# The query projection of a perceiver block as seven block products, with its block sums on VectorE

## The chip, the cores and the metric

The kernel runs on one core of one Trainium2 chip. The metric is the device time of one execution in microseconds (us), and lower is better. Before the change the median of three runs is 1107.33 us (1107.03 to 1108.09). The engines are called as in the profile: PE is TensorE (matmuls, with PEld for its weight loads), DVE is VectorE, ACT is ScalarE, POOL is GpSimd, and SP issues most transfers.

## The reference, cut to what matters

A block of 512 tokens, 512 wide, attends to a context of 8192 rows with 16 heads of 32; then a linear attention and a quantized feed-forward network follow. Everything is float32. The change touches only the queries of the first attention:

```python
x = x + xattn(layernorm(x), ctx_1024, ctx_1024, Wq, bq, Wk, bk, Wv, bv, Wo, bo)
# in it, with E = 512:
q = split_heads(query @ Wq + bq)      # 512 x 512 by 512 x 512
k = split_heads(key @ Wk + bk)        # 8192 x 512 by 512 x 512
v = split_heads(value @ Wv + bv)
weights = softmax(einsum('bhqd,bhkd->bhqk', q, k) / sqrt(32))
z = einsum('bhqk,bhkd->bhqd', weights, v)
```

## The kernel before, in words

The function `network` is built twice. The first copy (`exact` false) is the one that runs; the second (`exact` true) stands behind a test of a flag and is only run if the softmax's denominators fall out of their bounds. All that follows is the first copy.

The context is worked through in 16 blocks of 512 rows. Keys and values of a block are each a 512 x 512 x 512 product, made in `blockwise` (L441) as seven products of 256 x 256 x 256 blocks instead of eight (a Strassen scheme with 15 sums). `product` (L463) issues one of them in four steps, each with four matmuls of 32 output columns (`by_columns`, L385; two instructions per matmul in the profile, so 32 per product). `evict` (L487) adds a finished product into the result: on ACT for product 1 (L492), else on DVE with a plain addition (L479) or a pair of additions with the bias (L482). The products run in the order 1, 2, 6, 7, 5, 4, 3 (L527). Each takes a PSUM buffer from the pool `ps_m`, tag "pt", which has two, so a product needs the buffer of the second product before it to be evicted.

The sums that the scheme needs are made on POOL: four of a weight (`sums_of_weights`, L360, additions at L365) and four of a context block (`sums_of_ctx`, L373, additions at L383). Each is a 128x512 addition of tensors in SBUF.

The stretch around the change is straight-line code. In order: POOL gets the sums of Wk and of block 0 (L545, L546). PE makes ten matmuls of the identity, key product 1 of block 0 (L562), the transposes of the normed tokens `xn` into PSUM (L565), from where DVE and ACT copy them to `xnT` (L570, L572), and key product 2 (L573). Then come the queries (L574 to L579): for each of four groups of 128 columns `project` (L131) issues four full 128x128 matmuls of 512 columns (L136; 32 instructions in all) into a "pt" buffer, and ACT adds the bias into `qT` (L577). After that POOL gets the sums of Wv (L581), for which `place_w` takes the buffer of Wq, and the addition of `bo` to the residual (L583). The other five key products of block 0 follow on PE (L734), then `common_maxima` (L628), which reads `qT` for the first scores (L643) while the values of block 0 are made.

The helper `in_order` keeps the instructions of an engine in the order in which the code issues them. So what stands earlier in the code on DVE holds up what stands later on DVE, even where that is ready. Wq comes in one transfer of 1024 KB on SP's queue (L130), behind the halves of Wk and of context block 0.

Of the kernel before, what the change touches and what calls it, by code (L numbers as in the profile page):

```python
# [8 lines left out]
F32 = mybir.dt.float32  # L9
BF16 = mybir.dt.bfloat16  # L10
AF = mybir.ActivationFunctionType
ALU = mybir.AluOpType
# [4 lines left out]
P = 128  # L17
# [9 lines left out]
def network(  # L27
# [24 lines left out]
    nc = tc.nc  # L52
    S, E = x.shape
# [4 lines left out]
    NE = E // P  # L58
    NF = FF // P
    HG = P // D  # L60
    KB = 512
# [15 lines left out]
    def in_order(i):  # L77

        return tc.keep_in_program_order(i)
# [6 lines left out]
    for i in range(7):  # L86
        n = 1 << i
# [45 lines left out]
    def project(ps, lhsT, rhs):  # L133

        for c in range(NE):
            nc.tensor.matmul(  # L136
                ps, lhsT=lhsT(c), rhs=rhs(c), start=(c == 0), stop=(c == NE - 1)
            )
# [138 lines left out]
    ap2 = ctx.enter_context(tc.tile_pool(name="ap2", bufs=2))  # L277
    ap4 = ctx.enter_context(tc.tile_pool(name="ap4", bufs=4))
    ps_m = ctx.enter_context(tc.tile_pool(name="ps_m", bufs=2, space=PSUM))

    with ExitStack() as actx:
        aw = actx.enter_context(tc.tile_pool(name="aw", bufs=1))

        qT = aw.tile([P, NE, S], F32, name="qT")
# [11 lines left out]
        bias = aw.tile([P, NE], F32, name="bias")  # L296
# [4 lines left out]
        ct, kT, vt, tt = {}, {}, {}, {}  # L301
# [18 lines left out]
        wq_sb, wv_sb, wk_sb = place_w(), place_w(), place_w()  # L320
# [8 lines left out]
        bk_sb = load_cols(bk, NE, "bk_sb")  # L329
        load_w(Wq, wq_sb)  # L330
        bq_sb = load_cols(bq, NE, "bq_sb")
# [12 lines left out]
        xnT = ap4.tile([P, NE, S], F32, name="xnT", tag="ex")  # L344
# [11 lines left out]
        def block_of(w, i, j):  # L356

            return w[:, ts(j, NE // 2), ts(i, E // 2)]
# [79 lines left out]
                for k in range(NC) for c in range(NE)  # L438
            ]

        def blockwise(b, keys, parted=False):  # L441

            st = {"ps": {}}
            half = KB // 2

            def begin():
                if keys:
                    kT[b] = ap2.tile([P, NE, KB], F32, name="kT")  # L450
                    dst = kT[b]
                    st["C"] = {
                        (i, j): dst[:, ts(i, 2), ts(j, half)]
                        for i in range(2) for j in range(2)
                    }
                else:
                    vt[b] = ap2.tile([P, NC, E], F32, name="vt")
                    dst = vt[b]
                    st["C"] = {
                        (i, j): dst[:, ts(j, 2), ts(i, half)]  # L460
                        for i in range(2) for j in range(2)
                    }
            def product(n, m, k):  # L463
                w = (of_keys if keys else of_values)[n - 1]
                b11, _, b21, b22 = [
                    block_of(ct[b], kk, j) for j in range(2) for kk in range(2)
                ]
                t = tt[b]
                x = [b11, b21, b22, t[:, 3], t[:, 0], t[:, 1], t[:, 2]][n - 1]
                lhsT, rhs = (w, x) if keys else (x, w)  # L470
                by_columns(
                    st["ps"][n][:, m, :], lhsT[:, k, ts(m, P)], rhs[:, k, :],
                    k == 0, k == 1,
                )

            def add(dst, src, ps, i=None):

                if not keys or i is None:
                    in_order(nc.vector.tensor_tensor(dst, src, ps, ALU.add))  # L479
                    return  # L480
                for m in range(2):
                    in_order(nc.vector.scalar_tensor_tensor(  # L482
                        dst[:, m, :], ps[:, m, :], bk_sb[:, 2 * i + m : 2 * i + m + 1],
                        src[:, m, :], ALU.add, ALU.add,
                    ))

            def evict(n):  # L487
                C, ps = st["C"], st["ps"][n]

                C11, C12, C21, C22 = C[0, 0], C[0, 1], C[1, 0], C[1, 1]  # L490
                if n == 1:
                    in_order(nc.scalar.copy(C12, ps))  # L492
                elif n == 6:
                    add(C12, C12, ps)
                    if parted:
                        in_order(nc.scalar.copy(C21, C12))
                elif n == 7 and parted:
                    add(C22, C22, ps, 1)
                    add(C21, C21, ps, 1)
                elif n == 7:  # L500
                    add(C21, C12, ps, 1)
                elif n == 5 and parted:
                    add(C22, C12, ps)
                    add(C12, C12, ps, 0)
                elif n == 5:
                    add(C22, C21, ps)
                    add(C12, C12, ps, 0)
                elif n == 4:
                    add(C21, C21, ps)

                    if not keys:
                        sums_of_ctx(b + 1)
                elif n == 2:
                    add(C11, C12, ps, 0)
                elif n == 3:
                    add(C12, C12, ps)
                for i, j in {(7 if parted else 5): [(1, 1)], 4: [(1, 0)], 2: [(0, 0)], 3: [(0, 1)]}.get(n, []):
                    for m in range(2):
                        if keys:
                            made.add(("k", b, 2 * i + m, j))  # L520
                        else:
                            made.add(("v", b, 2 * j + m, i))
                if not keys and n == 3:
                    load_ctx(b + 2)

            steps = []
            for n in (1, 2, 6, 5, 3, 7, 4) if parted else (1, 2, 6, 7, 5, 4, 3):  # L527
                for m in range(2):
                    for k in range(2):
                        def step(n=n, m=m, k=k):  # L530
                            if (n, m, k) == (1, 0, 0):
                                begin()
                            if (m, k) == (0, 0):
                                ps = ps_m.tile([P, KB], F32, name="pm", tag="pt")
                                st["ps"][n] = ps.rearrange("p (a n) -> p a n", a=2)
                            product(n, m, k)
                            if (m, k) == (1, 1):
                                evict(n)
                        steps.append(step)
            return steps  # L540
# [3 lines left out]
        if not exact:  # L544
            of_keys = sums_of_weights(wk_sb)  # L545
# [3 lines left out]
        def first_keys(n):  # L549

            for step in key_steps[: 4 * n]:
                step()
            del key_steps[: 4 * n]

        with tc.tile_pool(name="ps_q", bufs=NE, space=PSUM) as ps_q:
# [12 lines left out]
            for c in range(NE):  # L568
                if c % 2 == 0:
                    in_order(nc.vector.tensor_copy(xnT[:, c, :], pts[c]))  # L570
                else:
                    in_order(nc.scalar.copy(xnT[:, c, :], pts[c]))  # L572
        first_keys(1)  # L573
        for g in range(NE):  # L574
            pq = ps_m.tile([P, S], F32, name="pq", tag="pt")
            project(pq, lambda c: wq_sb[:, c, ts(g, P)], lambda c: xnT[:, c, :])
            in_order(nc.scalar.activation(  # L577
                qT[:, g, :], pq, AF.Identity, bias=bq_sb[:, g : g + 1]
            ))  # L579
        if not exact:  # L580
            of_values = sums_of_weights(wv_sb)  # L581
        for t in range(NT):
# [8 lines left out]
        for b in range(first + 1, total):  # L591
# [5 lines left out]
            elif b < total - 1:  # L597

                steps = blockwise(b, True, True)
# [173 lines left out]
        def sums(dn, ex, start, stop):  # L773
            for j in range(HG):
                in_order(nc.tensor.matmul(
                    dn[ts(j, D), :], lhsT=ones_f, rhs=ex[:, j, :],
                    start=start, stop=stop,
                ))
# [90 lines left out]
        for i, u in enumerate(units):  # L869
            ex = weights(*u)  # L870
            if i >= last_block:
                b, g, k = u
# [25 lines left out]
            else:  # L898
# [3 lines left out]
                add = [weighted_sums(*late.pop(0)) for _ in range(len(late))]  # L902
# [116 lines left out]
    with ExitStack() as lctx:  # L1019
# [91 lines left out]
        def products(g):  # L1111


            ps = ps_m.tile([P, 2, F], F32, name="kv", tag="pt")
            for t in range(NT):
                for j in range(HG):
                    in_order(nc.tensor.matmul(
                        ps[ts(j, D), 0, :], lhsT=va[:, t, ds(g * P + j * D, D)],
                        rhs=kf[g][:, j, ts(t, F)],
                        start=(t == 0), stop=(t == NT - 1),  # L1120
                    ))
            for j in range(HG):
                in_order(nc.tensor.matmul(
                    ps[ts(j, D), 1, :], lhsT=ones_c, rhs=kf_sum[g][:, j, :],
                    start=True, stop=True,
                ))
            kvT[g] = lp.tile([P, 2, F], F32, name="kvT")
            in_order(nc.scalar.copy(kvT[g], ps))
# [215 lines left out]
    for q in range(NF // 4):  # L1344
# [14 lines left out]
        for i in range(4):  # L1359
            f = 4 * q + i  # L1360
# [7 lines left out]
            if f < 2 or i % 2 == 1:  # L1368
                k = f if f < 2 else f // 2 + 1
# [33 lines left out]
    for i in range(len(chunks) + 1):  # L1403
        if i < len(chunks):
            f, n = chunks[i]
# [4 lines left out]
        f, n = chunks[i - 1]  # L1410
# [77 lines left out]
```

## Time and profile before

| | us |
|---|---|
| median of three runs | 1107.33 |
| the profiled execution | 1107.43 |
| its span in the trace | 1105.6 |
| PE busy in the span | 1084.2 |
| DVE busy | 935.0 |
| ACT busy | 642.2 |
| POOL busy | 179.3 |
| queries on PE (L136), in the chain | 13.93, from 14.69 to 28.62 |
| the five key products after them | 8.94, from 28.62 |
| all before the chain reaches PE (start and first loads) | 9.00 |

The span is the time from the first to the last recorded instruction; the execution's own time is 1.8 us longer. "Busy" is the union of an engine's instruction times. The chain of work that ended last goes back from the last instruction to whatever released it, step by step. In rows of instructions, the duration of a single one can be longer than the distance to the next, since neighbours on an engine overlap a little.

### The profile page before, as it was taken

The page shows a single profiled execution, that of the slowest core. Times are in us where ns is not written, and L with a number is a line of the kernel's source. Part 1 is how long each engine was busy: PE and PEld are TensorE (multiplying, and loading weights), DVE is VectorE, ACT ScalarE, POOL GpSimd, SP SyncE. Part 2 cuts the span into 40 slices and gives each one's busy share as a digit, 9 for nine tenths or more (in the row PEclk, how much of TensorE's full clock was granted, in tenths as well). Part 3 has the DMA queues.
Part 4 walks back from the last instruction along what each step waited for, and adds up shares of the span by engine and source line. Part 5 has one row for each costly group of instructions (what it writes and reads, how often), then busy time and mean ns, then how long its engine had stood idle before and what let it go on. Part 6 is the DMA issues. An engine that isn't in the chain of part 4 may idle for free.

```text
span 1105.6 us, 30940 instructions
## 1 busy us (share of the span) xinstructions
PE 1084.2 (98%) x14272; PEld 409.9 (37%) x14272; DVE 935.0 (85%) x869; ACT 642.2 (58%) x434; POOL 179.3 (16%) x90
## 2 busy tenths in 40 slices
PE   8999999999999999999999999999999998999996
PEld 5443333333333333333333333333333322344342
DVE  3699999998988888888888888888889789666896
ACT  2465555566666766667665555555565666346353
POOL 3520303011403030303030302021120000013000
PEclk9999999999999999999999999999999999999998
DMA  7031212110302121212010101010101021040001
GB/s 267 14 104 41 96 56 81 59 59 31 97 31 69 52 75 31 68 59 68 30 59 2 41 2 40 2 40 2 40 2 40 2 77 39 1 190 2 1 1 42
DMA packets 24778, 55.56 MB, mean 50 GB/s; under 512 B 1984, under 2 KB 2496, under 8 KB 24384
## 3 DMA queue, kind: packets, MB, share of 16 engines
q1 hardware_dynamic: 24352, 52.97, 14.4%
q8 instruction: 114, 1.87, 0.7%
q10 hardware_dynamic: 288, 0.52, 0.1%
q14 instruction: 24, 0.20, 0.1%
HBM read 48.25 MB, written 5.24 MB: 48 GB/s over the span
## 4 chain that ended last, share of the span: by engine, by line
PE 91%; DVE 3%; ACT 3%; issue 1%; DMA 1%; SPq 0%; ACTq 0%; DVEq 0%
PE pm L388 37%; PE sc L818 24%; PE av L757 19%; ACT ex L827 3%; PE pq L1039 3%; PE po L930 1%; PE pq L136 1%; DVE unchanged L143 1%; PE pv L968 1%; PE pys L1389 1%; DMA ct<-in_ctxT 1%; DVE de L1155 1%; PE att L1144 1%; PE scm L643 0%; PE pk L388 0%
## 5 line engine op out<-in xcount | busy, mean ns | idle before, releaser
L827 ACT ACTIVATE ex<-sc,bias 128x2048 f32<-128x2048 f32 x252 | 496.3, 1970 | 339.9 <-PE sc L818 339.9
L836 DVE TENSOR_TENSOR acc<-acc,ex 128x2048 f32<-128x2048 f32 x248 | 585.0, 2359 | 67.3 <-ACT ex L827 66.7
L818 PE MATMUL sc<-qT,kT 32*64 32x512 f32 x4032 | 280.7, 613 | 4.8 <-ACT ex L827 4.8
L757 PE MATMUL av<-ex,vt 128*32 128x512 f32 x2048 | 266.9, 593 | 0.0
L383 POOL TENSOR_TENSOR tt<-ct 128x512 f32<-128x512 f32 x32 | 61.8, 1931 | 570.0 <-DMA ct<-in_ctxT 469.1
L818 PEld LDWEIGHTS sc<-qT,kT 32*64 32x64 f32 x4032 | 58.7, 129 | 217.0 <-ACT ex L827 194.4
L388 PE MATMUL pm<-w,tt 128*32 128x256 f32 x2048 | 126.8, 382 | 0.0
L388 PE MATMUL pm<-tt,w 128*32 128x256 f32 x1920 | 118.4, 382 | 0.0
L388 PE MATMUL pm<-w,ct 128*32 128x256 f32 x1536 | 96.6, 383 | 0.0
L479 DVE TENSOR_TENSOR vt<-vt,pm 128x512 f32<-128x512 f32 x112 | 75.4, 685 | 21.6 <-PE pm L388 20.6
L388 PE MATMUL pm<-ct,w 128*32 128x256 f32 x1440 | 90.3, 383 | 1.5 <-DMA ct<-in_ctxT 1.5
L388 PEld LDWEIGHTS pm<-w,tt 128*32 128x32 f32 x2048 | 59.7, 109 | 85.2 <-issue 51.8
L383 POOL TENSOR_TENSOR tt<-ct,tt 128x512 f32<-128x512 f32 x32 | 87.4, 2731 | 1.3
L757 PEld LDWEIGHTS av<-ex,vt 128*32 128x32 f32 x2048 | 65.3, 110 | 55.5 <-issue 14.0
L388 PEld LDWEIGHTS pm<-tt,w 128*32 128x32 f32 x1920 | 56.3, 109 | 78.9 <-issue 47.8
L388 PEld LDWEIGHTS pm<-w,ct 128*32 128x32 f32 x1536 | 43.6, 109 | 72.4 <-issue 47.0
L388 PEld LDWEIGHTS pm<-ct,w 128*32 128x32 f32 x1440 | 41.3, 109 | 67.3 <-issue 45.0
L479 DVE TENSOR_TENSOR kT<-kT,pm 128x512 f32<-128x512 f32 x60 | 40.9, 681 | 26.9 <-PE pm L388 26.1
L769 DVE TENSOR_TENSOR Z<-Z,av 128x512 f32<-128x512 f32 x64 | 43.4, 679 | 0.4 <-PE av L757 0.4
L482 DVE SCALAR_TENSOR_TENSOR kT<-pm,bk_sb,kT 128x256 f32<-128x256 f32 x92 | 39.9, 475 | 3.0 <-PE pm L388 1.0
L1061 ACT ACTIVATE er<-feat 128x1024 f32<-128x1024 f32 x32 | 30.2, 1029 | 11.3 <-PE feat L1083 6.4
L1067 DVE SCALAR_TENSOR_TENSOR f<-er 128x1024 f32<-128x1024 f32 x16 | 19.6, 1240 | 12.2 <-ACT er L1061 12.2
(184 smaller groups left out, 603.4 us busy)
## 6 DMA issues: line engine op xcount, KB each, us to landing
ct<-in_ctxT SPq DMA_DIRECT2D x15, 1024.0 KB, 5.3
wraw<-in_W1T SPq DMA_DIRECT2D x16, 512.0 KB, 3.8
wraw<-in_W2T SPq DMA_DIRECT2D x16, 512.0 KB, 3.8
wd<-wquant SPq DMA_DIRECT2D x16, 256.0 KB, 2.4
w_q<-wd SPq DMA_DIRECT2D x2, 2048.0 KB, 9.9
w<-in_w_qkv SPq DMA_DIRECT2D x3, 1024.0 KB, 5.0
w<-in_Wk SPq DMA_DIRECT2D x2, 512.0 KB, 6.6
ct<-in_ctxT SPq DMA_DIRECT2D x2, 512.0 KB, 7.6
```

The source lines that it names most:

```text
L383: in_order(nc.gpsimd.tensor_tensor(tt[b][:, i], x, y, ALU.subtract))
L388: in_order(nc.tensor.matmul(ps[ts(j, D)], lhsT=lhsT[:, ts(j, D)], rhs=rhs, start=start, stop=stop))
L479: in_order(nc.vector.tensor_tensor(dst, src, ps, ALU.add))
L482: in_order(nc.vector.scalar_tensor_tensor(dst[:, m, :], ps[:, m, :], bk_sb[:, 2 * i + m : 2 * i + m + 1], src[:, m, :], ALU.add, ALU.add,))
L757: in_order(nc.tensor.matmul(av[g][ts(j, D), :], lhsT=vt[b][:, k, ds(g * P + j * D, D)], rhs=ex[:, j, :], start=start, stop=stop,))
L769: in_order(nc.vector.tensor_tensor(Z[:, g, :], Z[:, g, :], ps, ALU.add))
L818: in_order(nc.tensor.matmul(sc[ts(h, P // 2), j, :], lhsT=kT[b][rows, g, ds(k * P + h * P // 2, P // 2)], rhs=qT[rows, g, :], start=not ex ...
L827: in_order(nc.scalar.activation(ex, sc, AF.Exp, bias=bias[:, g : g + 1], scale=SCALE))
L836: in_order(nc.vector.tensor_tensor(acc[:, g], acc[:, g], ex, ALU.add))
L1039: in_order(nc.tensor.matmul(ps, lhsT=wt[:, c, ts(g, P)], rhs=ynT[:, c, :], start=(c == 0), stop=(c == NE - 1),))
L1061: in_order(nc.scalar.activation(er[-1][:, d].rearrange("p a n -> p (a n)"), ps[h], function))
L1067: in_order(nc.vector.scalar_tensor_tensor(f[h], er[i][:, 0].rearrange("p a n -> p (a n)"), 1.0, er[i][:, 1].rearrange("p a n -> p (a n)"), ...
```

## The change

The queries are made by `blockwise` too, with a new flag `queries`: products of blocks of Wq with blocks of `xnT`, evicted into `qT` with the bias `bq`. The weights' sums `dw` and the tokens' sums `dx` (two tiles of the pool `ap4`, tag "ex") are eight additions of 128x512, issued on DVE between the other steps: two of the weights before key product 2, then two of the tokens, then one of each, then query products 1 and 2, then one of each again, then the other five products. The exact copy keeps the old form.

```diff
-        def blockwise(b, keys, parted=False):
+        def blockwise(b, keys, parted=False, queries=False):
...
                 if keys:
-                    kT[b] = ap2.tile([P, NE, KB], F32, name="kT")
-                    dst = kT[b]
+                    if not queries:
+                        kT[b] = ap2.tile([P, NE, KB], F32, name="kT")
+                    dst = qT if queries else kT[b]
...
             def product(n, m, k):
-                w = (of_keys if keys else of_values)[n - 1]
+                if queries:
+                    w, moving, t = of_queries[n - 1], xnT, of_tokens
+                else:
+                    w = (of_keys if keys else of_values)[n - 1]
+                    moving, t = ct[b], tt[b]
                 b11, _, b21, b22 = [
-                    block_of(ct[b], kk, j) for j in range(2) for kk in range(2)
+                    block_of(moving, kk, j) for j in range(2) for kk in range(2)
                 ]
-                t = tt[b]
...
                     in_order(nc.vector.scalar_tensor_tensor(
-                        dst[:, m, :], ps[:, m, :], bk_sb[:, 2 * i + m : 2 * i + m + 1],
+                        dst[:, m, :], ps[:, m, :],
+                        (bq_sb if queries else bk_sb)[:, 2 * i + m : 2 * i + m + 1],
                         src[:, m, :], ALU.add, ALU.add,
                     ))
...
-        first_keys(1)
-        for g in range(NE):
-            pq = ps_m.tile([P, S], F32, name="pq", tag="pt")
-            project(pq, lambda c: wq_sb[:, c, ts(g, P)], lambda c: xnT[:, c, :])
-            in_order(nc.scalar.activation(
-                qT[:, g, :], pq, AF.Identity, bias=bq_sb[:, g : g + 1]
-            ))
+        if exact:
...
+        else:
+            a11, a12, a21, a22 = [
+                block_of(wq_sb, i, j) for i in range(2) for j in range(2)
+            ]
+            b11, b12, b21, b22 = [block_of(xnT, k, j) for j in range(2) for k in range(2)]
+            of_weights, of_tokens = [
+                ap4.tile([P, 4, 2, E // 2], F32, name=f"of_{n}", tag="ex") for n in "wx"
+            ]
+            dw, dx = of_weights, of_tokens
+            of_queries = [a11, a12, dw[:, 3], a22, dw[:, 0], dw[:, 1], dw[:, 2]]
+
+            def sums(*ops):
+                for dst, x, y, how in ops:
+                    in_order(nc.vector.tensor_tensor(dst, x, y, how))
...
+            steps = blockwise(None, True, queries=True)
+
+            def products(n):
+                for _ in range(4 * n):
+                    steps.pop(0)()
+
+            add, sub = ALU.add, ALU.subtract
+            sums((dw[:, 0], a21, a22, add), (dw[:, 1], dw[:, 0], a11, sub))
+            first_keys(1)
+            sums((dx[:, 0], b12, b11, sub), (dx[:, 1], b22, dx[:, 0], sub))
+            sums((dw[:, 2], a11, a21, sub), (dx[:, 2], b22, b12, sub))
+            products(2)
+            sums((dw[:, 3], a12, dw[:, 1], sub), (dx[:, 3], b21, dx[:, 1], sub))
+            products(5)
```

Product n multiplies entry n of `of_queries` with entry n of the list in `product`: b11, b21, b22, t3, t0, t1, t2, where t is `of_tokens`. So products 1 and 2 need no sum, product 6 needs dw1 and dx1, product 7 dw2 and dx2, product 5 dw0 and dx0, product 4 dx3, and product 3 dw3.

More of the change, by code (lines that the diff above doesn't have):

```diff
@@ L518, in evict @@
                     for m in range(2):
-                        if keys:
+                        if queries:
+                            pass
+                        elif keys:
                             made.add(("k", b, 2 * i + m, j))
@@ L572, in network @@
                     in_order(nc.scalar.copy(xnT[:, c, :], pts[c]))
-        first_keys(1)
-        for g in range(NE):
-            pq = ps_m.tile([P, S], F32, name="pq", tag="pt")
-            project(pq, lambda c: wq_sb[:, c, ts(g, P)], lambda c: xnT[:, c, :])
-            in_order(nc.scalar.activation(
-                qT[:, g, :], pq, AF.Identity, bias=bq_sb[:, g : g + 1]
-            ))
+        if exact:
+            for g in range(NE):
+                pq = ps_m.tile([P, S], F32, name="pq", tag="pt")
+                project(pq, lambda c: wq_sb[:, c, ts(g, P)], lambda c: xnT[:, c, :])
+                in_order(nc.scalar.activation(
+                    qT[:, g, :], pq, AF.Identity, bias=bq_sb[:, g : g + 1]
+                ))
+        else:
[23 more added lines that the diff above has]
+            products(5)
         if not exact:
```

## The prediction

> **What bounds the kernel now.** I read the page first: busy time by engine, then the chain of work that ended last. Lines 1 and 2 show TensorE (PE) busy for 98% of the span and carrying 91% of the chain.
>
> ```profile
> PE 1084.2 (98%) x14272; PEld 409.9 (37%) x14272; DVE 935.0 (85%) x869; ACT 642.2 (58%) x434; POOL 179.3 (16%) x90
> ...
> PE 91%; DVE 3%; ACT 3%; issue 1%; DMA 1%; SPq 0%; ACTq 0%; DVEq 0%
> ```
>
> So a microsecond that PE gains or loses early is carried to the end, unless something else is late there. The change lies in the first 40 us, so next I read the chain in order of time there (start, length, what):
>
> ```profile
> 12.83 1.86 PE pm L388 x32
> 14.69 13.93 PE pq L136 x32
> 28.62 8.94 PE pm L388 x160
> ```
>
> The queries are the 13.93 us between key product 2 and the other five key products. Five products of 32 instructions take 8.94 us, 1.79 each. PE has no gap here. The table of stretches (PE, PEld, DVE, ACT, POOL busy, clock, DMA share, GB/s) says what else goes on:
>
> ```profile
> 14.60:28.60 14.00, 14.00 (x40) 6.05 (x40) 0.88 (x2) 2.06 (x3) 5.81 (x5) 1.00 0.57 199
> ```
>
> VectorE (DVE) is nearly idle, 0.88 of 14 us; GpSimd (POOL) works 5.81, and the timeline says when (start, length, engine, line):
>
> ```profile
> 10.37 5.10 POOL L365 TENSOR_TENSOR w<-w 128x512 f32<-128x512 f32 x4 [9.94 <-DMA w<-in_Wk]
> ...
> 12.54 1.29 DVE L570 COPY xnT<-pxt 128x512 f32<-128x512 f32 x2 [2.30 <-PE pxt L565]
> ...
> 14.84 0.88 DVE L482 SCALAR_TENSOR_TENSOR kT<-pm,bk_sb,kT 128x256 f32<-128x256 f32 x2 [1.02 <-issue]
> ...
> 15.41 1.27 POOL L383 TENSOR_TENSOR tt<-ct 128x512 f32<-128x512 f32 x1
> ...
> 16.77 1.27 POOL L383 TENSOR_TENSOR tt<-ct,tt 128x512 f32<-128x512 f32 x1
> ```
>
> POOL makes the key weights' sums (four) and block 0's sums (four, to 20.49) exactly where DVE is to make eight more. What that costs the trace shows later, where both engines add tensors that lie in SBUF:
>
> ```profile
> 119.96 1.28 POOL L383 TENSOR_TENSOR tt<-ct,tt 128x512 f32<-128x512 f32 x1
> 121.19 3.33 POOL L383 TENSOR_TENSOR tt<-ct 128x512 f32<-128x512 f32 x1
> 124.50 3.33 POOL L383 TENSOR_TENSOR tt<-ct,tt 128x512 f32<-128x512 f32 x1
> ```
> ```profile
> 120.56 2.83 DVE L836 TENSOR_TENSOR acc<-acc,ex 128x2048 f32<-128x2048 f32 x1
> 123.31 0.68 DVE L479 TENSOR_TENSOR kT<-kT,pm 128x512 f32<-128x512 f32 x1
> 123.91 2.78 DVE L836 TENSOR_TENSOR acc<-acc,ex 128x2048 f32<-128x2048 f32 x1
> ```
>
> Follow the ends: POOL 121.24, DVE 123.39, POOL 124.52, DVE 126.69, POOL 127.83. The steps are 2.15, 1.13, 2.17, 1.14: each ends one clean duration after the other's end. They do not run side by side; they take turns, and POOL's 3.33 is 2.2 of waiting and 1.13 of work. An instruction with a PSUM source takes no part: the key evictions at 30.55 to 33.2 keep their 0.69 and 0.88 beside POOL's L365 (28.70, four in 5.13, against 5.10 alone).
>
> **The change, step by step.** *Removed:* 32 query matmuls, 13.93 us of PE, and four ScalarE evictions of 0.69, which were beside PE. *Added on PE:* seven products at 1.79, 12.52 us. Alone that is 1.41 us gained. *Added on DVE:* eight sums of 128x512, and the evictions of six products (0.69 for an addition, 0.88 for a biased pair; pitch 0.60 and 0.86, since neighbours overlap). ScalarE evicts product 1.
>
> A sum alone costs 0.69 by the nearest row (two SBUF inputs, 128x512), 0.60 as pitch:
>
> ```profile
> L784 DVE TENSOR_TENSOR Z<-Z,acc 128x512 f32<-128x512 f32 x4 | 2.8, 692 | 0.1
> ```
>
> Taking turns, its own part is 2.17 - (2.28 - 0.69) = 0.58, scaled from the 128x2048 row (2.28 alone), and a POOL sum that goes before it costs 1.13.
>
> Three rules of the code turn DVE's time into PE waits. DVE keeps program order. The two "pt" PSUM buffers alternate, so a product waits for the eviction of the second one before it. And the sums are written ahead of evictions: dw0, dw1 (on the whole Wq) ahead of key product 2's, dx0, dx1, dw2, dx2 ahead of query product 2's, dw3, dx3 ahead of product 6's. Wq's row decides the start:
>
> ```profile
> w<-in_Wq SPq DMA_DIRECT2D x1, 1024.0 KB, 9.4
> ```
>
> Issued at 4.88, it lands at 14.28, after the xnT copies (13.83).
>
> DVE and POOL, by turns (ends in us): POOL's fourth L365 15.47; dw0 16.05; tt0 17.18; dw1 17.76; key eviction 18.6, with tt1 beside it to 18.89; dx0 19.47; tt2 20.60; dx1 21.18; tt3 22.31; dw2 22.89; dx2 23.5 (POOL is out of work); eviction of query product 2, 24.35; dw3 24.95; dx3 25.55; eviction of product 6, 26.15.
>
> PE (starts, products in the order 1, 2, 6, 7, 5, 4, 3): product 1 at 14.65; product 2 at 18.65, waiting for key product 2's buffer (2.2 idle); product 6 at 21.2, for dx1 (0.8 idle); product 7 at 24.4, for product 2's buffer (1.4 idle); product 5 at 26.2; 4 at 28.0; 3 at 29.8, its buffer free at 29.65. The rest of the keys starts at 31.6 where it started at 28.6: **+3.0 us**. The check: 1.41 gained, 4.4 of idle added.
>
> *What is moved and costs nothing.* POOL's sums of Wv wait for Wq's buffer; product 4 is its last reader, so they start at 29.8 instead of 28.70 and end at 34.9, beside five key products; values product 6 reads them first (45.05 before, 48 then). POOL's xs additions and block 1's sums follow some 1 us later, DVE then reading only PSUM. Without that cover block 1's sums would cost 1.13 a turn. The tt sums end at 22.3 instead of 20.5, needed at 31.6. Queries are read first some 8 us after the last eviction. No DMA issue is moved but behind PE.
>
> *Unknown prices.* (a) Eight sums of this shape beside POOL have no row: from 0.60 each (no turns) to 1.71 each (a turn every time); I take the turns counted above, five waits, since the L836 rows are the nearest. (b) Who goes next when both wait: if DVE kept its place for the independent pair dw2, dx2, tt3 would come behind them and in the gap of an eviction: product 7 at 23.25, end 30.7, +2.2. With hand-overs of 0.1 each, +3.8.
>
> The Trainium skill, SBUF — State Buffer, section "Who interferes with whom", says that a DVE instruction with two SBUF inputs contends with a GpSimd instruction that reads SBUF, and that the loser blocks for the whole instruction. The 2.15/1.13 steps agree; it speaks against these sums on DVE here, and against reading the overlap as half speed each, which would give +0.9. [...]
>
> (c) PE's clock is 1.00 in all stretches read, also in 5 to 9 us, where PE sat idle for 1.47. A gap of 2.2 us is not in these; I take no loss, and at worst the three gaps cost one product more, 1.8.
>
> TensorE: Matmul & The Clock Gate, Part 1, halves the clock after an idle window of about 3.4 us; by it no gap of mine would do that. If one did, an estimate from that page is 3.4 us at half speed, 1.7 us more. No row here shows it.
>
> **The rivals.**
>
> *The sums hide* (not slower). If they cost 0.60 each beside POOL, dw1 ends at 15.5, product 2 starts at 16.55, dx2 ends at 19.0, product 7 starts at 20.15 without waiting, and the last ends at 27.4: -1.2, **1106.2**. For it: DVE is idle there. Against: the turns. The point that decides: to end at 28.6, product 5 must start by 23.2, so product 6's eviction ends by 23.15; from 14.3, less evictions of 0.86, 0.86 and 0.60, eight sums have 6.5 us, 0.8 each. Mine average 1.2.
>
> *Both at half speed* (a shared, not an exclusive port): sums at 0.9, evictions untouched; product 7 starts at 21.6, the last ends at 29.5: +0.9, **1108.3**. For it: a 128x2048 addition is just 1.2 to 1.5 times as long beside POOL. Against: the clean steps of the ends.
>
> *More lost than counted*: hand-overs, a slower clock in the gaps, or a scores stage that starts worse; +4.7, **1112.1**. Nothing in the trace asks for it.
>
> *It doesn't do what it says*: the seven products replace all 32 matmuls in the path that runs; only the guarded second pass keeps them. So no chance of its own.
>
> **How the numbers follow.** The sum is against the profiled execution: 1107.43 us, its span 1105.6 and 1.8 around it; the runs' median is 1107.33, 0.1 below. 1107.43 + 3.0 = **1110.4**. Chances: turns as counted 0.62 (1109.8 to 1111.3); DVE keeps its place 0.12 (1109.6); half speed 0.08; hidden 0.08; more lost 0.10. The range of 8 in 10 leaves out the hidden case and the worst half of the last: 1108.2 to 1111.8. Within 0.2% (2.2 us, to 1109.55) is about what cannot be told from no change: half of the second case, half speed, hidden and a little of the first, 0.22; slower 0.74. Faster by 0.2% would need more than the 1.41 that PE can gain; 0.04 for what I have not seen.
>
> **What would show it.** Right: the sums on DVE with a mean near 1.2 us and a POOL end just before most; POOL's tt to about 22.3; PE idle for some 4.4 us between 16 and 25, waiting first for DVE's key eviction; the five key products from about 31.6. Wrong: sums near 0.7 while POOL works, or no PE gap; then the turns fail. If the gaps are there and the end is not later, something after 40 us had slack that I don't see.

## The result, and the profile after

The changed kernel takes 1109.91 us (median of 15 runs, 1109.47 to 1110.93); the kernel before, 1107.67 (15 runs, 1106.99 to 1110.04). The ratio of the means is 1.0016, 95% interval 1.0009 to 1.0023: slower by 1.0 to 2.5 us. The medians are 2.24 us apart and the means 1.79, because five of the 15 runs of before lie between 1109.27 and 1110.04. The profiled execution of the changed kernel took 1109.70, its span is 1107.9 (1105.6 before).

Page of the changed kernel, lines 1 and 4:

```profile
PE 1080.7 (98%) x14459; PEld 411.3 (37%) x14464; DVE 948.8 (86%) x887; ACT 639.6 (58%) x431; POOL 179.2 (16%) x90
...
PE 90%; DVE 4%; ACT 3%; DMA 1%; issue 1%; SPq 0%; ACTq 0%; DVEq 0%
```

PE is busy for 3.5 us less and DVE for 13.8 more, and the chain has moved from PE to DVE by a point. Most of PE's 3.5 is not the change's: 2.65 lie behind 980 us (113.78 to 111.13 us busy), in stages that it leaves as they were. Where, the chain in order of time says (start, length, what):

```profile
14.43 1.60 DVE of_w L601
16.03 0.02 issue
16.06 0.06 DVE of_w L601
16.12 1.50 issue
17.62 0.86 DVE kT L487 x2
```

Before, the chain ran through PE here without a gap. Now it runs through the sums; 1.50 us of the second one stand as "issue", time in which nothing that the profile shows is waited for. No semaphore stands for that wait, so the two timelines have to be laid side by side. DVE of the changed kernel (start, length):

```profile
14.43 1.59 DVE L601 TENSOR_TENSOR of_w<-w 128x512 f32<-128x512 f32 x1 [0.61 <-DMA w<-in_Wq]
16.06 1.64 DVE L601 TENSOR_TENSOR of_w<-of_w,w 128x512 f32<-128x512 f32 x1
...
20.99 1.76 DVE L601 TENSOR_TENSOR of_w<-w 128x512 f32<-128x512 f32 x1
22.67 0.68 DVE L601 TENSOR_TENSOR of_x<-xnT 128x512 f32<-128x512 f32 x1
```

POOL of the changed kernel:

```profile
15.43 1.72 POOL L383 TENSOR_TENSOR tt<-ct 128x512 f32<-128x512 f32 x1
17.23 1.59 POOL L383 TENSOR_TENSOR tt<-ct,tt 128x512 f32<-128x512 f32 x1
18.79 1.73 POOL L383 TENSOR_TENSOR tt<-ct 128x512 f32<-128x512 f32 x1
20.48 1.72 POOL L383 TENSOR_TENSOR tt<-ct,tt 128x512 f32<-128x512 f32 x1
```

Take the ends: DVE 16.02, POOL 17.15, DVE 17.70, and at the last turn POOL 22.20, DVE 22.75. POOL needs 1.13 from the end of DVE's sum, DVE 0.55 from the end of POOL's. Once POOL has no more work, DVE's next sum takes 0.68 (22.67). PE pays for it in three gaps:

```profile
18.63 1.93 PE L388 MATMUL pm<-xnT,w 128*32 128x256 f32 x32 [2.15 <-DVE kT L487]
21.21 1.93 PE L388 MATMUL pm<-of_x,of_w 128*32 128x256 f32 x32 [0.65 <-DVE of_x L601]
24.28 3.66 PE L388 MATMUL pm<-of_x,of_w 128*32 128x256 f32 x64 [1.14 <-DVE qT L487]
```

The five key products start at 31.34, where they started at 28.55: +2.79. From there the shift is carried: a weight chunk's load is issued at 55.41 instead of 52.69, a context block's at 566.41 instead of 563.70, the last weights' at 980.27 instead of 977.57, 2.70 to 2.72 throughout. The span differs by 2.3 only: on DVE the shift is 2.70 up to 1040 us and 2.35 from 1042.68 on. The stretches behind that, before and after (PE, PEld, DVE, ACT, POOL busy, clock, DMA share, GB/s):

```profile
1040.00:1060.00 20.00, 17.89 (x65) 9.34 (x65) 18.55 (x58) 5.92 (x9) 0.00 (x0) 0.91 0.00 0
```
```profile
1042.70:1062.70 20.00, 17.21 (x66) 8.11 (x67) 18.70 (x59) 5.89 (x9) 0.00 (x0) 1.00 0.00 1
```

The granted clock was 0.91 there before and 1.00 after, in a stage that the change leaves alone. But the clock did not shorten the span: it first fell at about 1054.6 us, when the shift was already 2.35, and the last transfers are issued 2.34 later than before. What differs ahead of 1042.68 is one idle time of DVE, 0.46 us before the instruction at 1042.34 (L1156) in the kernel before and 0.11 in the changed one. Why it differs is open.

### The profile page after: what moved, and what is told of

Same layout as the page of the kernel before. It is cut to its first block, busy times and chain, and to the rows that moved or that the text cites. A ratio compares the mean times of both kernels' runs of the same rounds, so it can differ in the third digit from the quotient of the medians.

```text
span 1107.9 us, 31341 instructions
## 1 busy us (share of the span) xinstructions
PE 1080.7 (98%) x14459; PEld 411.3 (37%) x14464; DVE 948.8 (86%) x887; ACT 639.6 (58%) x431; POOL 179.2 (16%) x90
## 4 chain that ended last, share of the span: by engine, by line
PE 90%; DVE 4%; ACT 3%; DMA 1%; issue 1%; SPq 0%; ACTq 0%; DVEq 0%
PE pm L388 37%; PE sc L857 24%; PE av L796 19%; ACT ex L866 3%; PE pq L1078 3%; PE po L969 1%; DVE unchanged L143 1%; PE pv L1007 1%; PE pys L1428 1%; DMA w<-in_Wq 1%; DVE de L1194 1%; PE att L1183 1%; PE scm L682 0%; PE pk L388 0%; PE dn L814 0%
```

## The experiments

The theory: DVE and POOL take turns at instructions that read SBUF, and DVE's sums lie ahead of evictions that PE waits for. Rival A: the order of sums and evictions on DVE makes the gaps, whatever a sum costs. Rival B: the sums are slow for another reason, such as loads that land then, or PE reading the same tiles.

Each ratio is to runs of the kernel before made beside that experiment (medians 1107.70 and 1107.80).

| kernel | five key products start, us | median, us | ratio to before |
|---|---|---|---|
| before | 28.55 | 1107.67 | |
| changed | 31.34 | 1109.91 | 1.0016 (1.0009 to 1.0023) |
| e1_pool_later | 27.33 | 1106.18 | 0.9986 (0.9977 to 0.9995) |
| e8_one_turn | 28.22 | 1106.92 | 0.9990 (0.9981 to 0.9999) |
| e9_pool_copies | 28.67 | 1107.37 (one run) | |
| e4_pool_writes | 27.30 | 1105.82 (one run) | |
| e6_sums_on_pool | 30.73 | 1109.54 | 1.0011 (1.0001 to 1.0020) |
| e2_evictions_first | 33.96 | 1112.16 | 1.0037 (1.0023 to 1.0051) |
| e7_kept_warm | 31.63 | 1110.48 | 1.0021 (1.0012 to 1.0031) |
| e5_pool_twice | 34.73 | 1112.44 | 1.0041 (1.0026 to 1.0057) |

**GpSimd later.** `hold` puts the fourth sum of Wk and block 0's four sums in a list that is issued behind VectorE's last sum; a one-element read of dx3 makes POOL wait.

```diff
-            of_keys = sums_of_weights(wk_sb)
-            sums_of_ctx(0)
+            of_keys = sums_of_weights(wk_sb, hold=True)
+            sums_of_ctx(0, hold=True)
...
+            in_order(nc.gpsimd.tensor_tensor(
+                tt[0][:, 0, 0, :1], dx[:, 3, 0, :1], dx[:, 3, 0, :1], sub
+            ))
+            while held:
+                held.pop(0)()
             products(5)
```

> The changed kernel, with GpSimd's fourth sum of Wk and its four sums of block 0 put behind VectorE's last sum (a one-element GpSimd read of dx3 ahead of them). VectorE's program order and TensorE's order stay. Theory (VectorE and GpSimd take turns at additions of two SBUF tensors): the eight sums take about 0.6 to 0.7 us each, back to back, TensorE waits under 0.5 us in all among the query products, and the five key products start at about 27.3 us instead of 31.4 (28.6 before the change): about 1.3 us below the kernel before, 1106.2. Rival A (the order of the evictions behind the sums makes the waits): the gaps of 2.15 and 1.14 us stay, and it is the time of the changed kernel less 1 us at most, 1109. Rival B (the sums are slow for another reason, the loads of Wv and block 1 that land until 20 us, or TensorE reading the same tiles): the sums stay at 1.6 us, and the time that of the changed kernel, 1109.9.

Measured: 1106.18 us. The timeline of DVE and that of PE in this kernel:

```profile
14.46 0.69 DVE L608 TENSOR_TENSOR of_w<-w 128x512 f32<-128x512 f32 x1 [0.55 <-DMA w<-in_Wq]
15.19 0.69 DVE L608 TENSOR_TENSOR of_w<-of_w,w 128x512 f32<-128x512 f32 x1
...
17.97 0.69 DVE L608 TENSOR_TENSOR of_w<-w 128x512 f32<-128x512 f32 x1
```
```profile
16.81 1.94 PE L395 MATMUL pm<-xnT,w 128*32 128x256 f32 x32 [0.31 <-DVE kT L494]
18.53 5.39 PE L395 MATMUL pm<-of_x,of_w 128*32 128x256 f32 x96
```

All eight sums take 0.68 or 0.69 with DVE's order unchanged and the same loads and matmuls beside them, and of PE's three gaps one of 0.31 is left. That refutes rival B, and of rival A leaves the 0.31. This kernel is below both others, the one before included, though by 0.14% only.

**Evictions first.** GpSimd's work stays; on DVE each eviction moves ahead of the sums that held it. `blockwise` hands out its `evict`, and the steps of products 2 and 6 no longer call it themselves.

```diff
...
+            first_keys(1)
             sums((dw[:, 0], a21, a22, add), (dw[:, 1], dw[:, 0], a11, sub))
-            first_keys(1)
             sums((dx[:, 0], b12, b11, sub), (dx[:, 1], b22, dx[:, 0], sub))
+            products(2)
+            evict_query(2)
             sums((dw[:, 2], a11, a21, sub), (dx[:, 2], b22, b12, sub))
-            products(2)
+            products(1)
+            evict_query(6)
             sums((dw[:, 3], a12, dw[:, 1], sub), (dx[:, 3], b21, dx[:, 1], sub))
-            products(5)
+            products(4)
```

> The changed kernel with the evictions moved ahead on VectorE: key product 2's ahead of dw0 and dw1, query product 2's ahead of dw2 and dx2, query product 6's ahead of dw3 and dx3. GpSimd's work stays where it is. Theory of turns: the first gap (2.15 us ahead of query product 2) goes, but the four GpSimd sums of block 0 are still in turn with dw0, dw1, dx0, dx1, so dx1 ends at about 22.3 us instead of 21.07, product 6 waits for it, and the five key products start at about 31.5: within 0.3 us of the changed kernel. Rival A (order): both long gaps go, the key products start at about 28.5 or earlier, 3 us below the changed kernel. Rival B: with sums of 1.6 us one after the other, as in the theory.

Measured: 1112.16, 2.25 above the changed kernel: a miss for the theory's number and further from rival A. The first gap went and a single one of 4.24 us came, ahead of product 6, which starts at 22.83 (theory: 22.3, and loads landed some 0.5 us later in this execution). But then three products took 7.5 us (to 30.36) instead of 5.4:

```profile
22.83 7.72 PE L388 MATMUL pm<-of_x,of_w 128*32 128x256 f32 x96 [4.24 <-DVE of_x L603]
```

The stretches of this kernel show why, in the clock's column (1.00 up to 20.6):

```profile
20.60:21.60 1.00, 0.00 (x0) 0.00 (x0) 0.90 (x2) 0.00 (x0) 1.00 (x1) 0.60 1.10 341
21.60:22.20 0.60, 0.00 (x0) 0.00 (x0) 0.60 (x1) 0.00 (x0) 0.53 (x1) 0.50 0.69 183
...
24.80:25.80 1.00, 1.00 (x13) 0.46 (x9) 0.00 (x0) 0.00 (x0) 0.00 (x0) 0.50 0.00 0
```

PE's clock was halved in the gap, at about 20.8 (0.60 over the first of these stretches is full clock for 0.2 us and half for 0.8), and stayed so until about 27.6. The next run tells whether that is the whole of it.

**Kept warm.** The same, with matmuls of the identity in the gap:

```diff
             products(2)
+            with tc.tile_pool(name="ps_k", bufs=1, space=PSUM) as ps_k:
+                idle = ps_k.tile([P, P], F32, name="idle")
+                for _ in range(16):
+                    in_order(nc.tensor.matmul(
+                        idle, lhsT=ident, rhs=ident, start=True, stop=True
+                    ))
             evict_query(2)
```

> The run with the evictions first, with sixteen matmuls of the identity (32 instructions, about 3.4 us, into a PSUM buffer that nothing reads) put into TensorE's gap of 4.24 us ahead of query product 6. That run was 2.2 us slower than the theory of turns gave, and its trace shows three products in 7.7 us instead of 5.4 and a granted clock of 0.50 behind the gap. If the clock is the cause: the products behind the gap take 1.79 us each again, the key products start at 31.3 to 31.8, and the time is that of the changed kernel, 1109.9 to 1110.3, about 2 us below the run with the evictions first, though more work is done. If the moved evictions themselves cost the 2.2 us: it stays at 1112.

Measured: 1110.48, key products at 31.63. PE's timeline and the stretch behind the gap:

```profile
18.27 3.84 PE L621 MATMUL idle<-ident 128*128 128x128 f32 x32
22.58 5.65 PE L388 MATMUL pm<-of_x,of_w 128*32 128x256 f32 x96 [0.47 <-DVE of_x L603]
28.02 1.94 PE L388 MATMUL pm<-of_x,w 128*32 128x256 f32 x32
```
```profile
22.60:26.20 3.60, 3.55 (x64) 2.32 (x68) 3.45 (x7) 0.00 (x0) 0.00 (x0) 1.00 0.03 10
```

The clock is 1.00 and three products take 5.4 us (22.58 to 28.02). So the clock cost the missing 2 us, and with it out of the way the moved evictions leave the kernel about where it was (1109.91): the order is not what costs.

**A double dose.** Block 0's sums made twice by POOL (`] * times` on the list of the four, with 2 for block 0).

> The changed kernel, with GpSimd's four sums of block 0 made twice over (same result). Theory of turns: the second four are in turn with dx2, dw3 and dx3 too, about 1.13 us each, less what lies beside an eviction: about 2.5 us later than the changed kernel, 1112.4, key products from about 34. Rival B (something other than GpSimd slows the sums): dx2, dw3 and dx3 stay at 0.68 us, no change against the changed kernel. Rival A (order): the same as rival B.

Measured: 1112.44, +2.5. The timelines show a second POOL sum and the new waits of DVE where the changed kernel had 0.68:

```profile
22.68 1.71 POOL L383 TENSOR_TENSOR tt<-ct 128x512 f32<-128x512 f32 x1
```
```profile
23.19 1.75 DVE L601 TENSOR_TENSOR of_x<-xnT 128x512 f32<-128x512 f32 x1
...
26.54 1.75 DVE L601 TENSOR_TENSOR of_x<-xnT,of_x 128x512 f32<-128x512 f32 x1
```

The key products' 34.73 is not clean: this one execution took 1113.5, its first key product ran for 3.55 us instead of 1.93, and the clock fell to 0.50 behind a gap of 2.21. So dw0 came late here (15.84), waited for nobody (0.68), and seven of the eight sums were in turn.

**One turn left.** As GpSimd later, but with the fourth sum of Wk at its old place (`of_keys = sums_of_weights(wk_sb)`).

> As the run with GpSimd's sums late, but the fourth sum of Wk stays where it was, so that one turn is left: dw0 waits for it until 15.45. Theory of turns: dw0 takes 1.6 us, the other seven sums 0.7; product 2 starts at 17.55 instead of 16.81, product 5 waits for product 6's eviction at 22.7, and the key products start at about 28.4: 1.1 us above the run with GpSimd's sums late, 1107.2, about the kernel before. Rival (the turns are a wait only while several GpSimd sums are queued): as with all sums late, 1106.2.

Measured: 1106.92. POOL's sums of Wk and dw0:

```profile
12.98 2.52 POOL L367 TENSOR_TENSOR w<-w 128x512 f32<-128x512 f32 x2
```
```profile
14.84 1.21 DVE L608 TENSOR_TENSOR of_w<-w 128x512 f32<-128x512 f32 x1 [0.98 <-DMA w<-in_Wq]
```

dw0 takes 1.21, having come at 14.84 in this execution, and ends at 16.05, 0.55 behind POOL's end at 15.50; the other seven take 0.68 or 0.69. A single sum in POOL's hands is waited for, so the rival falls. The doses stand in order: no turn 1106.18, one 1106.92, five 1109.91, seven or eight 1112.44. Between the first two it is the trace that decides and not the time: their runs overlap (1105.52 to 1107.28, and 1106.25 to 1107.52), and of the 0.89 us between their key products 0.36 are a later Wq (query product 1 at 14.95 instead of 14.59).

**What of POOL's work takes turns.** GpSimd later, with twelve memsets (or, in the second run, six copies) by POOL in the time that it is idle:

```diff
+            for i in range(12):
+                in_order(nc.gpsimd.memset(tt[0][:, i % 4], 0.0))
```
```diff
+            for i in range(6):
+                j, k = divmod(i % 4, 2)
+                in_order(nc.gpsimd.tensor_copy(tt[0][:, i % 4], block_of(ct[0], k, j)))
```

> As the first run (GpSimd's sums behind VectorE's), but GpSimd makes twelve memsets of 128x512 into the tile of block 0's sums in that time, from about 14.2 us on; the sums overwrite it later. Does GpSimd's work as such hold VectorE up, or its reading of SBUF? If only the reads do: VectorE's sums stay at 0.6 to 0.7 us beside the memsets, key products from about 27.3 us. If any access of GpSimd does: each sum waits for a memset, and the start comes later by about eight times a memset's duration, at most.

> As the run with memsets beside VectorE's sums, but with six GpSimd copies of a 128x512 block of the context into the tile of block 0's sums, from 14.2 us on. They read one SBUF tensor where the memsets read none. If GpSimd's reads are what takes turns with VectorE's second input: the sums wait for the copies as they do for additions, each by about a copy's duration, as far as there are copies; the key products start later than 27.3. If only two-input GpSimd instructions do: sums of 0.69 us as with the memsets.

With the memsets, POOL and DVE in their timelines:

```profile
14.27 5.60 POOL L563 MEMSET tt<- 128x512 f32 x12
```
```profile
16.56 0.68 DVE L610 TENSOR_TENSOR of_x<-xnT 128x512 f32<-128x512 f32 x1
```

With the copies:

```profile
14.30 5.23 POOL L564 COPY tt<-ct 128x512 f32<-128x512 f32 x6
```
```profile
18.98 1.09 DVE L611 TENSOR_TENSOR of_w<-w 128x512 f32<-128x512 f32 x1
```

Beside the memsets each sum takes 0.68 or 0.69. Beside the copies the first five take 0.86 to 1.09, and the sixth, when the copies are done, 0.68; the key products start 1.4 us later. The two kernels ran once each, and it is these durations that carry the reading, not the times. So it is POOL's reading of SBUF that takes turns, with one input or two. The Trainium skill says the same in SBUF — State Buffer, section "Who interferes with whom": a VectorE instruction with two SBUF inputs contends with a GpSimd instruction that reads SBUF, not with one that only writes it. These two runs agree.

**The sums on GpSimd.** `nc.vector` becomes `nc.gpsimd` in `sums`, and block 0's sums follow theirs.

> The changed kernel with the eight sums of the queries on GpSimd instead of VectorE, behind its sums of Wk and ahead of its sums of block 0. So no additions of two SBUF tensors run on VectorE there, and no engine takes turns, but GpSimd needs 1.25 us for a sum where VectorE alone needs 0.6. Theory of turns: dx1 ends at about 20.6, dx2 at 23.1, product 3 at 30.3, so the five key products start at about 30.3 instead of 31.4: 1.1 us below the changed kernel and 1.7 above the kernel before, 1109.0 (up to 1110 if a gap of 2.4 us lowers TensorE's clock as in the run with the evictions first). Rival A (order): with all evictions in time on VectorE it would be as fast as the run with GpSimd's sums late, 1106.2.

Measured: 1109.54. PE's timeline:

```profile
21.19 1.93 PE L388 MATMUL pm<-of_x,of_w 128*32 128x256 f32 x32 [2.53 <-POOL of_x L601]
23.66 3.66 PE L388 MATMUL pm<-of_x,of_w 128*32 128x256 f32 x64 [0.54 <-POOL of_x L601]
```

POOL's sums take 1.26 to 1.28 each, nobody waits for a turn, and PE waits 2.53 and 0.54 us for dx1 and dx2; key products at 30.73, with the first key product of the block 0.5 us late in this execution. All evictions were in time and it is still 3.4 us above GpSimd later: evictions in time are not enough where the sums themselves come late, against rival A's 1106.2. The clock stayed at 1.00. The median is 0.37 below the changed kernel, with overlapping intervals.

## Why the prediction was right, and where it was not

The forecast was 1110.4, range 1108.2 to 1111.8; measured 1109.91.

- *What PE gains.* 1.41 us were taken. In GpSimd later, from query product 1 (14.59) to the key products (27.33) are 12.74 us with a gap of 0.31, against 13.93 before: 1.19 kept, 1.50 without the gap. Right.
- *The turns.* Foreseen ends: dw0 16.05, dw1 17.76, dx1 21.18, dw2 22.89. Measured: 16.02, 17.70, 21.07, 22.75. A POOL sum in turn was put at 1.13 and measured 1.13, a DVE sum at 0.58 and measured 0.55. The mean of the eight is 1.20, foreseen "near 1.2".
- *Who goes next.* The one that has waited longer: tt3, issued at 20.48, went before dw2, issued at 20.99. The case in which DVE keeps its place is excluded; in the double dose all pairs alternate, and a POOL sum issued at 22.68 went before dx2, issued at 23.19. Whether it is waiting time that decides or strict alternation can't be told here, since both name the same engine each time.
- *The gaps.* Foreseen 2.2, 0.8 and 1.4, counted from one product's start to the next less 1.79. Counted so, they measured 2.30, 0.79 and 1.28, which is 4.37 in all against 4.4; the profile's own idle times, 2.15, 0.65 and 1.14, begin 0.14 later, at the end of a product that nothing follows (1.93). The key products started at 31.34, not 31.6, from small things: query product 1 started at 14.54 instead of 14.65, the seven products took 12.43 instead of 12.52, and the biased eviction, taken as 0.86, holds the next instruction up for 0.79 (17.62 to 18.41, 23.27 to 24.06).
- *Carried to the end.* 2.71 us from 52 to 980 us; nothing had slack there. The last 0.4 went in one idle time of DVE at 1042 us, which the sum had no term for; the change is not known to have a part in it.
- *The clock.* No loss was taken for gaps of about 2 us, and in the changed kernel none came. That was closer than it looked: see the last section.
- *The chances.* This is the step that fits least. "Slower by over 0.2%" had 0.74, and the ratio is 1.0016 with an interval that ends at 1.0023: that it is over 0.2% is not shown. The sum was set against one execution of 1107.43 and three runs near it, while five of the 15 runs of before lie about 2 us higher and the mean of the 15 is 1108.2. A shift of 2.7 us in the trace became 1.8 in the ratio of means. The spread of the kernel before belonged in the chances, not only the spread of my steps.

The rival *both at half speed* fell with the ends of the turns, *the sums hide* became true in GpSimd later: 1106.18 where 1106.2 was given, once the condition (sums under 0.8 each) holds.

## What to carry to other kernels

Before work is moved to an idle VectorE, lay its timeline over GpSimd's: here additions of two SBUF tensors on VectorE waited for GpSimd's additions and copies out of SBUF (the two kinds that were tried), whole instruction by whole instruction, and the wait stood in the instruction's own duration and as "issue" in the chain. Moving GpSimd's work past the spot by a real dependency was worth 3.7 us here; moving VectorE's evictions was worth nothing. And if instructions wait in TensorE's path, the sum can have two parts: the gap, and the clock behind it.

## What the runs showed of the hardware that was not expected

The granted clock of TensorE fell to 0.50 behind a gap of 4.24 us (evictions first), some 2.2 us into it, and cost 2 us more; and behind a gap of 2.21 us with gaps of 0.63 and 0.65 ahead of it (double dose), some 0.6 us after PE had gone back to work at 25.87:

```profile
24.70:25.20 0.50, 0.00 (x0) 0.00 (x0) 0.50 (x2) 0.00 (x0) 0.50 (x1) 1.00 0.00 0
25.20:25.90 0.70, 0.03 (x4) 0.06 (x5) 0.70 (x3) 0.00 (x0) 0.70 (x1) 1.00 0.00 0
25.90:27.40 1.50, 1.50 (x20) 0.98 (x24) 1.50 (x2) 0.00 (x0) 1.50 (x2) 0.69 0.04 11
27.40:28.40 1.00, 1.00 (x16) 0.54 (x8) 1.00 (x2) 0.00 (x0) 1.00 (x2) 0.50 0.00 0
```

It did not fall behind gaps of 2.15 and 1.14 (changed kernel) or 2.53 and 0.54 (sums on GpSimd). The kernel before has such a fall too, 0.50 from about 1054.6 to 1058.0 us, behind a gap of 1.41 with shorter ones after it; the changed kernel, with a gap of 1.05 in that place, has none. The Trainium skill, TensorE: Matmul & The Clock Gate, Part 1, asks for an idle window of about 3.4 us; the gap of 2.21 shows that a single gap can be shorter, and these runs do not settle what decides. In the double dose's execution the first key product took 3.55 us instead of 1.93, a single matmul 632 ns instead of 379, although the clock's column shows 1.00 there: slow matmuls near the start need not show in that column. Whether the runs of before near 1109.5 have the same cause was not tried.
